# Score products of a cross-attention kernel: one row group per round takes 128 query rows at once

## The chip, the core and the metric

The kernel runs on one core of a Trainium2 chip. The metric is device time in microseconds (us) of that core for one execution. The kernel before takes 506.81 us, the median of three executions (506.36, 506.81 and 507.71).

## What is computed

One cross-attention layer with a residual and a layer norm, all in float32: 4 batches of 2048 query rows and 77 context rows, width 512, 16 heads of 32.

```python
qs  = (q @ wq).reshape(4, 2048, 16, 32).transpose(0, 2, 1, 3)
ks_ = (k @ wk).reshape(4,   77, 16, 32).transpose(0, 2, 1, 3)
vs  = (v @ wv).reshape(4,   77, 16, 32).transpose(0, 2, 1, 3)
scores = jnp.einsum('bhqd,bhkd->bhqk', qs, ks_) / jnp.sqrt(32.)
scores = jnp.where(mask[:, None, :, :], -jnp.inf, scores)
attn = jnp.einsum('bhqk,bhkd->bhqd', jax.nn.softmax(scores, -1), vs)
out  = attn.transpose(0, 2, 1, 3).reshape(4, 2048, 512) @ wo + q
out  = (out - mean) / jnp.sqrt(var + 1e-5) * gamma + beta
```

## The kernel before, in words

The 8192 query rows are cut into 64 tiles of 128 rows. Two tiles make a block, four tiles a group. For a group, TensorE (PE) makes the queries with `q_visit` (operand names pq<-xth, xtl; each product is three products of split high and low parts, rows L190 and L192). For a tile it makes the scores (`score`, L321, names sc<-kct,q). VectorE (DVE) adds the mask and finds each head's maximum (`maxima`, L364), ScalarE (ACT) takes the exponentials with their sums (`exps`, L379), GpSimd (POOL) divides by the sums (`normalise`, L390), DVE turns the probabilities by 32x32 squares (`transp`, L413), and DMAs regroup them (`regroup_part`, L425). PE then multiplies them with the values (`av`, L459, names pa<-PT,vsb) and the result with the output weights (`o_proj`, L564, names po<-woh, wol). What follows is the residual, the layer norm and the store.

The heads are 32 wide, so a query tile lies on PE's 128 contraction rows as four heads, each on its own 32 rows: a **row group**, `j` = 0 to 3. There are four such sets of heads, `g` = 0 to 3, so a tile has 4 x 4 scores of 128 query rows by 77 keys. In `score` the queries are the weights (loaded into the array), the keys are what streams through it. In the kernel before, each score is made in two products of 64 query rows, `half` = 0 and 64; each uses an array section of 32 rows by 64 columns, which the profile writes as 32*64. A **round** is one trip through the four row groups, with both halves: eight products. Because the data are float32, the trace has two loads and two MATMUL records for each product, so a round is 16 records, a tile 64 and a block 128.

Each engine runs its instructions in the order in which the program writes them. Nothing but two tables of words sets that order: the first six tiles come from a loop, the next 24 blocks (tiles 6 to 53) from `PAIR`, the last ten tiles from `ORDER`. A visit to the scores is one stretch on PE. For the 16 single tiles it is `scores`: four rounds. For the 24 blocks it is `scores_pair` (word S: six rounds) and `scores_rest` (word D: two rounds, their row groups taken as 0 and 2, then 3 and 1); but for the first of these blocks the two follow directly on each other on PE. Ahead of a block's visit PE does `av`, behind it `o_proj`.

The scores go to PSUM banks: one per row group for a single tile (sc_0 to sc_3), and for a block four of its own and two shared ones (sc_e, sc_f). DVE reads them from there.

Of the kernel before, what the change touches and what calls it, by code (L numbers as in the profile page):

```python
# [17 lines left out]
P = 128  # L18
# [8 lines left out]
GH = 4  # L27
# [49 lines left out]
def xattn_layernorm(  # L77
# [29 lines left out]
    def bank(name):  # L107
        while len(ring) % 8 in kept:
            ring.append(ring[-8])
        ring.append(ring[-8] if kept else ps.tile([P, 512], F32, tag="mm", name=name))  # L110
        return ring[-1]
# [49 lines left out]
    def keys_of(h):  # L161
        return slice(TAIL_K, NK2) if h % 2 == 0 else slice(0, NK)
# [145 lines left out]
    def scores(t):  # L308
        nmax[t] = sb.tile([P, H], F32, tag="nm", bufs=3, name=f"nm_{t}")
        sums[t] = sb.tile([P, H], F32, tag="sum", bufs=3, name=f"sum_{t}")  # L310
        sc = [bank(f"sc_{t}_{j}") for j in range(GH)]
        scs[t] = {(g, j): sc[j][:, g * NK : (g + 1) * NK] for g in range(NG) for j in range(GH)}
        for g in range(NG):
            for half in range(0, P, P // 2):
                for j in range(GH):
                    score(t, g, j, half, P // 2)

    def score(t, g, j, r0, n):
        q = slice(HD * j, HD * (j + 1))
        at = (t % 4) * P + r0  # L320
        nc.tensor.matmul(  # L321
            scs[t][g, j][r0 : r0 + n],
            qd[t // 4][q, g, at : at + n],
            kct[q, g, t // TPB, keys_of(j)],
            start=True,
            stop=True,
        )

    def scores_pair(b):
        for t in (2 * b, 2 * b + 1):  # L330
            nmax[t] = sb.tile([P, H], F32, tag="nm", bufs=3, name=f"nm_{t}")
            sums[t] = sb.tile([P, H], F32, tag="sum", bufs=3, name=f"sum_{t}")
            scs[t] = {}
        own = [bank(f"sc_{b}_{j}") for j in range(GH)]
        both = [bank(f"sc_{b}_{j}") for j in ("e", "f")]
        units = []
        for j in range(GH):
            mine = [(2 * b, g) for g in range(NG)] + [(2 * b + 1, g) for g in range(NG)]
            for i, (t, g) in enumerate(mine):
                bk, at = (own[j], i) if i < 6 else (both[j // 2], 2 * (j % 2) + i - 6)  # L340
                scs[t][g, j] = bk[:, at * NK : (at + 1) * NK]
            units.append(mine[6:] + mine[:6] if j % 2 == 0 else mine)
        for i in range(6):
            for half in range(0, P, P // 2):
                for j in range(GH):
                    score(*units[j][i], j, half, P // 2)
        held[b] = units

    def scores_rest(b):
        units = held.pop(b)  # L350
        for i in (6, 7):
            for js in ((0, 2), (3, 1)):
                for half in range(0, P, P // 2):
                    for j in js:
                        score(*units[j][i], j, half, P // 2)

    def maxima(t, lo, hi):
        pb = pbuf[t % NPB]
# [410 lines left out]
    for u in range(0, JOIN, 2):  # L769
# [6 lines left out]
        for t in (u - 4, u - 3):  # L776
            if t >= 0:
                load_x(t)
        scores(u)
        maxima(u, 0, H // 2)  # L780
        if u == 2:
# [53 lines left out]
        if u >= 4:  # L835
            av(n - 2)
            av_hi(n - 2, 0)
            av_hi(n - 2, 1)
        scores(u + 1)
        maxima(u + 1, 0, H // 4)  # L840
        if u >= 4:
# [42 lines left out]

    tile_ops = {
        "S": scores, "r": recip, "n": normalise, "t": transp, "W": av_tile, "x": load_x, "O": o_proj,
        "X": lambda t: resid(t, range(NC_D // 2 if t == NT - 1 else NC_D)), "+": residual, "u": rsqrt_one, "y": centre, "z": finish, "k": scale, "f": affine, "w": store,
        "v": bias_one, "K": stretch, "G": shift, "p": pool_scale, "I": act_mean, "J": act_squares, "M": keep,
# [48 lines left out]
    def pair(n):  # L937
        u = 2 * n
        words = PAIR.split()
        if n == JOIN // 2:  # L940
            words.remove("O-6")
            words.insert(words.index("D"), "O-6")
        for word in words:
            op, k, part, queue = read(word)
            if op == "S":
                scores_pair(n)
            elif op == "D":
                scores_rest(n)
            elif op in "LB":
                m, at = divmod(u, TPB)  # L950
                if m + 1 < NB and op == "L" and at == TPB - 10:
                    load_mask(m + 1)
                elif m + 1 < NB and op == "B" and at >= TPB - 8:
                    mask_quarter(m + 1, (at - TPB + 8) // 2)
            elif op == "P" and "." not in word:
                regroup(n + k)
            elif op in "Qq":
                if op == "Q" or divmod(2 * n + k, 4) in qp:
                    do(op, 2 * n + k)
            elif op in "gij":  # L960
                do(op, n + k)
            elif op in "PVab":
                if op in "PV" or n + k > JOIN // 2 - 3:
                    do(op, n + k, part, queue)
            elif u + k >= 0:
                do(op, u + k, part, queue)
# [54 lines left out]
```

## Time and profile before

| | |
|---|---|
| median of three executions | 506.81 us |
| the profiled execution's own time | 508.02 us |
| its span in the profile | 506.2 us |
| PE busy | 497.0 us (98%) |
| PE's weight loads (PEld) busy | 391.7 us (77%) |
| DVE, ACT, POOL busy | 463.0, 473.0, 427.6 us (91%, 93%, 84%) |
| records of the score products (L321) | 4096, in 58.48 us |

Busy time counts the stretches in which at least one instruction of an engine is under way; products overlap, so a busy PE need not be at its peak. A form such as 32*64 is the section of the array (contraction rows by weight columns), and what follows it is what streams (32 partitions by 77 elements). A line of the chain of waits is a share of the span on the path that ended last. PEclk is the share of TensorE's clock that was granted.

### The profile page before, as it was taken

Reading aid. Unit: us, or ns where it says so; the run is one execution under the profiler, and the core shown is the slowest. Engines: PE = TensorE matmul, PEld = TensorE weight load, DVE = VectorE, ACT = ScalarE, POOL = GpSimd, SP = SyncE. Lnnn points to the kernel's source line nnn. Section 1 sums busy time; section 2 is a strip of 40 time slices with the busy share of each in tenths; the row PEclk is TensorE's granted clock in tenths of the full one; section 3 lists DMA queues with packets and bytes.
Section 4 is the critical chain, followed back from the end, with each engine's and each line's share of the span. In section 5 each row is a group of like instructions: output and inputs, shape, how many; then the busy total and the mean of one; then the engine's idle time right before and its main releaser. Section 6 shows DMA issues by size and latency. Waiting matters only on the chain.

```text
span 506.2 us, 20441 instructions
## 1 busy us (share of the span) xinstructions
PE 497.0 (98%) x6908; PEld 391.7 (77%) x6908; DVE 463.0 (91%) x2567; ACT 473.0 (93%) x2240; POOL 427.6 (84%) x384
## 2 busy tenths in 40 slices
PE   9999999999999999999999999999999999999995
PEld 7987678777777877777787777778777777777784
DVE  6698899999989988999998998999999889999997
ACT  6798899999999999999999999999999999999971
POOL 0559367989988988989998888999988888999995
PEclk9999999999999999999999999999999999999998
DMA  8945867677887778878777877877778787677665
GB/s 314 388 168 149 222 187 194 190 196 202 231 229 218 223 201 219 229 209 229 213 219 211 232 199 223 229 224 227 216 196 221 199 247 235 170 189 222 167 210 208
DMA packets 58280, 109.50 MB, mean 216 GB/s; under 512 B 9203, under 2 KB 10739, under 8 KB 58176
## 3 DMA queue, kind: packets, MB, share of 16 engines
q1 hardware_dynamic: 55776, 103.35, 71.7%
q0 software_dynamic: 1872, 4.20, 2.8%
q8 instruction: 55, 0.90, 0.8%
q10 hardware_dynamic: 528, 0.66, 0.4%
q14 instruction: 49, 0.40, 0.3%
HBM read 41.68 MB, written 16.78 MB: 115 GB/s over the span
## 4 chain that ended last, share of the span: by engine, by line
PE 79%; DVE 8%; ACT 7%; DMA 2%; issue 1%; SPq 1%; POOL 0%; POOLq 0%; DVEq 0%; ACTq 0%
PE pq L192 27%; PE po L564 26%; PE pa L459 10%; ACT pbuf L379 7%; PE sc L321 6%; DVE B L413 2%; PE sc L564 2%; DVE pbuf L364 2%; PE sc_e L321 2%; PE pk L218 1%; PE pq L725 1%; PE pq L190 1%; PE sc_f L321 1%; SPq L425 1%; DMA out<-o 1%
## 5 line engine op out<-in xcount | busy, mean ns | idle before, releaser
L379 ACT ACTIVATE pbuf<-pbuf,nm 128x77 f32<-128x77 f32 x1024 | 352.6, 349 | 8.6 <-DVE nm L364 7.8
L379 ACT ACTIVATION_READ_ACCUMULATOR pbuf<-pbuf,nm 128x1 f32 x1024 | 193.9, 189 | 0.0
L390 POOL TENSOR_TENSOR pbuf<-pbuf,ri 128x1232 f32<-128x1232 f32 x63 | 145.9, 2316 | 20.8 <-DVE ri L385 17.4
L364 DVE CUSTOM_DVE_ANT_0 pbuf<-sc,mb 128x77 f32<-128x77 f32 x828 | 143.9, 231 | 6.9 <-PE sc L321 6.4
L192 PE MATMUL pq<-xtl,wqh 128*128 128x512 f32 (+1 forms) x256 | 98.3, 384 | 0.0
L192 PE MATMUL pq<-xth,wql 128*128 128x512 f32 (+1 forms) x256 | 98.2, 384 | 0.0
L413 DVE STREAM_TRANSPOSE B<-pbuf 128x1280 f32<-128x1280 f32 x63 | 94.6, 1503 | 0.4
L564 PE MATMUL po<-woh,AH 128*128 128x512 f32 x224 | 90.7, 405 | 0.0
L192 PE MATMUL pq<-xth,wqh 128*128 128x512 f32 (+1 forms) x230 | 88.6, 385 | 0.0
L564 PE MATMUL po<-wol,AH 128*128 128x512 f32 x224 | 87.3, 390 | 0.0
L592 POOL TENSOR_TENSOR o<-o,gam 128x512 f32<-128x512 f32 x53 | 68.7, 1295 | 21.5 <-ACT o L588 21.5
L564 PE MATMUL po<-woh,AL 128*128 128x512 f32 x224 | 86.5, 391 | 0.0
L364 DVE DVE_READ_ACCUMULATOR2_ANT nm<- 128x1 f32 x1024 | 84.4, 82 | 0.0
L593 POOL TENSOR_TENSOR o<-o,bet 128x512 f32<-128x512 f32 x53 | 68.3, 1289 | 4.2
L180 POOL TENSOR_TENSOR xtl<-xtf,xth 128x1024 fp32r<-128x1024 f32 x28 | 67.4, 2409 | 0.1
L459 PE MATMUL pa<-PT,vsb 96*32 96x256 f32 x960 | 58.2, 382 | 1.6 <-DVE vsb L267 1.0
L321 PE MATMUL sc<-kct,q 32*64 32x77 f32 x3312 | 56.0, 238 | 0.5 <-DVE q L209 0.5
L192 PEld LDWEIGHTS pq<-xth,wql 128*128 128x128 f32 x256 | 48.2, 188 | 8.4
L192 PEld LDWEIGHTS pq<-xtl,wqh 128*128 128x128 f32 x256 | 48.1, 188 | 8.4
L321 PEld LDWEIGHTS sc<-kct,q 32*64 32x64 f32 x3312 | 49.3, 130 | 6.5 <-issue 4.4
L564 PEld LDWEIGHTS po<-woh,AH 128*128 128x128 f32 x224 | 42.0, 188 | 10.7 <-DVE nm L364 0.4
L192 PEld LDWEIGHTS pq<-xth,wqh 128*128 128x128 f32 x230 | 43.2, 188 | 9.0
(191 smaller groups left out, 855.1 us busy)
## 6 DMA issues: line engine op xcount, KB each, us to landing
PT<-B SPq DMA_DIRECT2D x355, 128.0 KB
xtf<-xT SPq DMA_DIRECT2D x28, 512.0 KB
o<-x SPq DMA_DIRECT2D x56, 256.0 KB
out<-o SPq DMA_DIRECT2D x56, 256.0 KB
PT<-B POOLq DMA_DIRECT2D x16, 128.0 KB, 4.5
o_end<-x SPq DMA_DIRECT2D x7, 256.0 KB
out<-o_end SPq DMA_DIRECT2D x7, 256.0 KB
xtf<-xT SPq DMA_DIRECT2D x4, 256.0 KB
```

The costliest lines, as they stand in the source:

```text
L180: nc.gpsimd.tensor_tensor(l, fx.pop((g, c)), h.bitcast(F32), ALU.subtract)
L190: nc.tensor.matmul(pq[:, cols], wc, r[:, c, cols], start=False, stop=False)
L192: nc.tensor.matmul(pq, wc, r[:, c, rs], start=(n == 0), stop=(n == 11))
L321: nc.tensor.matmul(scs[t][g, j][r0 : r0 + n], qd[t // 4][q, g, at : at + n], kct[q, g, t // TPB, keys_of(j)], start=True, stop=True,)
L364: nc.vector.tensor_tensor_reduce(pb[:, i // 2, (i % 2) * NK : (i % 2 + 1) * NK], scs[t][g, j], mb[:, t % TPB, keys_of(h)], -1.0, CEIL, ALU ...
L379: nc.scalar.activation(p, p, AF.Exp, bias=nmax[t][:, i : i + 1], scale=-1.0, accum_out=sums[t][:, i : i + 1])
L390: nc.gpsimd.tensor_tensor(pv, pv, rv.to_broadcast((P, NP, 2, NK)), ALU.mult)
L413: nc.vector.transpose(bt.rearrange("p c q r -> p q c r"), pbuf[t % NPB].rearrange("p q (c r) -> p q c r", c=5),)
L459: nc.tensor.matmul(pas[b, g // 2][HD * j : HD * (j + 1), (g % 2) * BLK : (g % 2 + 1) * BLK], vsb[:, 2 * b // TPB, HD * h : HD * (h + 1)], ...
L564: nc.tensor.matmul(pos[t], a[:, c, rs], w[:, c], start=(first and n == 0), stop=(n == 11))
L592: nc.gpsimd.tensor_tensor(o, o, gam, ALU.mult)
L593: nc.gpsimd.tensor_tensor(o, o, bet, ALU.add)
```

## The change

In each round, one of the four row groups makes its score in one product with all 128 query rows as weights (a section of 32 rows by 128 columns) in place of the two halves. Which one moves on with the round: row group `j == g` for a single tile, `j == i % 4` for round `i` of a block. The product stands where the first half stood; the second half is left out. A round so has seven products in place of eight. What is multiplied and where it is written stay the same.

```diff
         for g in range(NG):
             for half in range(0, P, P // 2):
                 for j in range(GH):
-                    score(t, g, j, half, P // 2)
+                    score_part(t, g, j, half, j == g)
...
+    def score_part(t, g, j, half, whole):
+        if not whole:
+            score(t, g, j, half, P // 2)
+        elif half == 0:
+            score(t, g, j, 0, P)
...
         for i in range(6):
             for half in range(0, P, P // 2):
                 for j in range(GH):
-                    score(*units[j][i], j, half, P // 2)
+                    score_part(*units[j][i], j, half, j == i % GH)
...
             for js in ((0, 2), (3, 1)):
                 for half in range(0, P, P // 2):
                     for j in js:
-                        score(*units[j][i], j, half, P // 2)
+                        score_part(*units[j][i], j, half, j == i % GH)
```

On PE, a single tile's first two rounds stood so before (sc_0 to sc_3 are the banks of row groups 0 to 3; 64x77 is 64 weight columns and 77 streamed keys):

```order
L321 MATMUL sc_0_358<-kct,q_131 64x77 [waits Activation_49]
L321 MATMUL sc_1_359<-kct,q_131 64x77 [waits Activation_49]
L321 MATMUL sc_2_360<-kct,q_131 64x77
L321 MATMUL sc_3_361<-kct,q_131 64x77 [waits PE_49]
L321 MATMUL sc_0_358<-kct,q_131 64x77
L321 MATMUL sc_1_359<-kct,q_131 64x77
L321 MATMUL sc_2_360<-kct,q_131 64x77
L321 MATMUL sc_3_361<-kct,q_131 64x77
L321 MATMUL sc_0_358<-kct,q_131 64x77 [waits DVE_49]
L321 MATMUL sc_1_359<-kct,q_131 64x77 [waits DVE_49]
L321 MATMUL sc_2_360<-kct,q_131 64x77
L321 MATMUL sc_3_361<-kct,q_131 64x77
```

With the change, the same place, from the visit's first product into its third round:

```order
L321 MATMUL sc_0_358<-kct,q_131 128x77 [waits Activation_49]
L321 MATMUL sc_1_359<-kct,q_131 64x77 [waits Activation_49]
L321 MATMUL sc_2_360<-kct,q_131 64x77
L321 MATMUL sc_3_361<-kct,q_131 64x77 [waits PE_49]
L321 MATMUL sc_1_359<-kct,q_131 64x77
L321 MATMUL sc_2_360<-kct,q_131 64x77
L321 MATMUL sc_3_361<-kct,q_131 64x77
L321 MATMUL sc_0_358<-kct,q_131 64x77 [waits DVE_49]
L321 MATMUL sc_1_359<-kct,q_131 128x77 [waits DVE_49]
L321 MATMUL sc_2_360<-kct,q_131 64x77
L321 MATMUL sc_3_361<-kct,q_131 64x77
```

Seven products with 64 columns stand between one with 128 and the next. At the end of a block's visit, with the change (rounds 6 and 7 of `scores_rest` and the first product of `o_proj`, which is L570 there):

```order
L321 MATMUL sc_2_2883<-kct,q_2265 128x77
L321 MATMUL sc_0_2881<-kct,q_2265 64x77
L321 MATMUL sc_f<-kct,q_2265 64x77 [waits DVE_49]
L321 MATMUL sc_e<-kct,q_2265 64x77
L321 MATMUL sc_f<-kct,q_2265 64x77
L321 MATMUL sc_e<-kct,q_2265 64x77
L321 MATMUL sc_0_2881<-kct,q_2265 64x77
L321 MATMUL sc_2_2883<-kct,q_2265 64x77
L321 MATMUL sc_0_2881<-kct,q_2265 64x77
L321 MATMUL sc_2_2883<-kct,q_2265 64x77
L321 MATMUL sc_f<-kct,q_2265 128x77
L321 MATMUL sc_e<-kct,q_2265 64x77 x2
```

Here nine products with 64 columns stand between two with 128, and two behind the last. Over the whole program 256 products with 128 columns take the place of 512 with 64; PE goes from a 64-column product to a 128-column one 216 times, and back 256 times. On the other engines no instruction is added, removed or moved.

## The prediction

> **What bounds the kernel now.** I read the page's busy times and chain first, then the busy times of the steady stretch, then PE's waits.
>
> ```profile
> PE 497.0 (98%) x6908; PEld 391.7 (77%) x6908; DVE 463.0 (91%) x2567; ACT 473.0 (93%) x2240; POOL 427.6 (84%) x384
> PE 79%; DVE 8%; ACT 7%; DMA 2%; issue 1%; SPq 1%; POOL 0%; POOLq 0%; DVEq 0%; ACTq 0%
> ...
> 105.80:253.10 147.30, 147.30 (x2094) 115.48 (x2090) 137.73 (x786) 144.75 (x691) 133.46 (x111) 1.00 0.78 216
> ...
> PE pa L459 <- DVE vsb L267: 1.0, 1, 1.0
> PE pw L692 <- POOL ident L683: 0.9, 1, 0.9
> PE sc L321 <- DVE q L209: 0.5, 1, 0.5
> PE pa L459 <- DVE ri L385: 0.3, 1, 0.3
> ```
>
> PE holds 79% of the chain. The third row is ten block periods (columns: PE, PEld, DVE, ACT, POOL): PE never rests, ACT (fourth) leaves 2.55 us, 0.255 us a period. Over the whole run PE waits 1.8 us for DVE (three rows; pw is the warm-up). So whatever a score visit costs on PE, the kernel pays nearly in full; what it saves, up to 0.255 us a block, before ACT is as full as PE.
>
> What the visits cost now, by the busy times of the score products alone (columns: PE, PEld) over the span and over 21 block visits, and a single tile's visit in the timeline (columns: start, time from the first start to the last end, count):
>
> ```profile
> 0.00:506.20 506.20, 58.48 (x4096) 51.91 (x4096) 1.00 0.76 216
> 91.00:400.00 309.00, 37.50 (x2688) 34.22 (x2688) 1.00 0.78 217
> ...
> 418.58 0.39 PE L564 MATMUL po<-woh,AL 128*128 128x512 f32 x1
> 418.90 0.95 PE L321 MATMUL sc<-kct,q 32*64 32x77 f32 x64
> 419.78 0.50 PE L192 MATMUL pq<-xth,wqh 128*128 128x512 f32 x1
> 420.11 0.39 PE L192 MATMUL pq<-xtl,wqh 128*128 128x512 f32 x1
> ...
> L321 PE MATMUL sc<-kct,q x3312: 222/225/277, 20.9 to 471.6; 32*64 32x77 f32 x195
> ```
>
> A single visit takes 0.88 us from its first start to the next work's (418.90 to 419.78). Its last record starts at 418.90 + 0.95 - 0.225 (last row, median), so 0.155 us pass from the last score's start to the first start in the next form. Busy time runs 0.225 - 0.155 = 0.07 us past that; a block's visit is 37.50 / 21 - 0.07 = 1.72 us. All visits: 16 x 0.88 + 24 x 1.72 = 55 us. That is all there is to gain from.
>
> **What a change of form costs.** The question is what happens between 32*64 and 32*128, which no row of this trace shows. Other changes of form it shows in plenty:
>
> ```profile
> 252.79 0.38 PE L459 MATMUL pa<-PT,vsb 96*32 96x256 f32 x1
> 253.10 0.28 PE L321 MATMUL sc_e<-kct,q 32*64 32x77 f32 x1
> ...
> 253.15 0.28 PE L321 MATMUL sc<-kct,q 32*64 32x77 f32 x1
> 253.22 0.23 PE L321 MATMUL sc_e<-kct,q 32*64 32x77 f32 x1
> ...
> 253.27 0.23 PE L321 MATMUL sc<-kct,q 32*64 32x77 f32 x1
> 253.29 0.23 PE L321 MATMUL sc_e<-kct,q 32*64 32x77 f32 x1
> ...
> 483.85 0.38 PE L459 MATMUL pa<-PT,vsb 96*32 96x256 f32 x1
> 484.15 0.44 PE L439 MATMUL pa<-ident,pbuf 128*77 128x128 f32 x2
> ...
> 492.73 0.27 PE L492 MATMUL po<-PT,vsb 96*32 96x128 f32 x1
> 492.82 0.28 PE L474 MATMUL sc<-PT,vsb 77*32 77x128 f32 x1
> ```
>
> Within one form, eight scores on eight sections start 0.007 us apart (253.10 to 253.15, eight starts), the second pass of the same product comes 0.12 later (253.22), the next product on that section 0.065 after that (253.29): a pass streams 0.065. When the form changes, nothing overlaps: 0.155 from the last start is 0.065 of streaming and 0.09 in which PE starts nothing. From pa to the scores it is 0.31. At 483.85 the columns go from 32 to 77 and the rows from 96 to 128, both sides float32: again 0.30. At 492.73 the rows go from 96 to 77 and the columns stay 32: 0.09, no gap. So the gap follows the columns of the section, and 64 to 128 of them at equal rows is such a change. [...]
>
> Behind a gap the first load is bare too: the first MATMUL of a 32*64 stretch takes 0.277 against 0.225, so 0.05, that of 128 columns 0.50 against 0.39 (rows at 419.78 and 420.11), so 0.11.
>
> **The price of a round, step by step.** The 128-column product (W): load 0.11, then its second load, streaming of the second pass, gap. The loads follow each other at once here:
>
> ```profile
> 419.78 0.19 PEld L192 LDWEIGHTS pq<-xth,wqh 128*128 128x128 f32 x1
> 419.88 0.19 PEld L192 LDWEIGHTS pq<-xtl,wqh 128*128 128x128 f32 x1
> ```
>
> The second load starts 0.10 behind the first, while the first product still streams through the same rows. Two loads of 0.10 to 0.11 let W's second pass start 0.215 after its first load, and 0.155 later the halves may load: 0.37 for W. I bound it by 0.275 (loads as short as the 0.05 of 64 columns: 0.05 + 0.07 + 0.155) and 0.43 (second load only after the first pass, 0.065 more). I take 0.37, from the rows with 128 columns. [...]
>
> Seven halves: all on different sections, so second passes start from 0.12 on, the last at 0.12 + 6 x 0.007 = 0.16, and 0.155 later W may load: 0.315. Bounds: 0.27 (no spacing) and 0.40 (products let in at the visit's average, 1.72 / 64 = 0.027 each: 7 x 0.027 + 0.05 + 0.155). Likewise 0.28 for two halves, 0.29 for three, 0.31 for six; nine use one section twice, 0.41.
>
> A single tile: four W, three times seven halves, then three: 4 x 0.37 + 3 x 0.315 + 0.29 = 2.72 in place of 0.88, +1.84. A block: eight W, and 7, 7, 7, 3, 7, 6, 9, 2 halves: 2.96 + 4 x 0.315 + 0.29 + 0.31 + 0.41 + 0.28 = 5.51 in place of 1.72, +3.79. The eight saved products are in that. Sum: 16 x 1.84 + 24 x 3.79 = 29.4 + 91.0 = 120.4. PE's waits of 1.8 for DVE may take up to that much; I subtract 1.8. It all lies on PE, which has no other cover; a block's 14.7 us period becomes 18.5, and ACT, DVE and POOL, which were close behind, get slack. Maxima start later by part of the visit, but the exponentials behind them have that slack. The waits stand on the same products as before; a W that writes a bank waits for DVE once in place of twice. DMA issues do not move.
>
> Against the profiled execution's 508.0: 508.0 + 118.6 = 626.6. It was 1.2 above the median, so **625 us**. With the lower bounds a tile is 2.2 (+1.3) and a block 4.4 (+2.7), 85.6 less 1.8: 591. With the upper, 3.1 (+2.2) and 6.5 (+4.8): 150, 657.
>
> **Rivals.**
>
> No gap between these two forms (faster). For it: rows stay 32 wide, and no row shows this pair; halves run out of each other's order as if sections were independent. A visit then only loses records, 16 of 128 in a block (1.72 / 8 = 0.215) and 8 of 64 in a single (0.11): 24 x 0.215 + 16 x 0.11 = 6.9 us, 500 us. ACT's 0.255 a block just allows that. Against: 483.85, where columns alone made the gap.
>
> The gap is local: W waits for its own row group, the other three go on. For it: each form change in the trace involves sections that share rows, so none shows whether unshared rows wait. Then one row group sets the pace: over a single tile, three rounds of 0.13 and one W of 0.37 with 0.09 ahead and a bare load of 0.05 behind: 0.90 against 0.88. A block: 6 x 0.13 + 2 x 0.51 = 1.80 against 1.72. 16 x 0.02 + 24 x 0.08 = 2.2: 509 us, no change or a little slower. Against: the first scores at 253.10 need 64 of the columns, yet none starts before all of pa is through.
>
> The clock: PE streams less in visits three times as long and its clock is cut.
>
> ```profile
> 492.00:494.00 2.00, 2.00 (x65) 1.80 (x66) 2.00 (x4) 1.53 (x4) 1.84 (x4) 1.00 0.58 223
> 502.00:504.00 2.00, 0.00 (x0) 0.00 (x0) 0.60 (x2) 0.00 (x0) 0.90 (x1) 0.84 0.43 152
> 504.00:506.20 2.20, 0.00 (x0) 0.00 (x0) 0.00 (x0) 0.00 (x0) 0.00 (x0) 0.50 0.26 101
> ```
>
> The clock falls to 0.50 only where PE has nothing for some four us; with small products and form changes (492 to 494) it stays at 1.00. If visits of 5.51 and 2.72 ran with loads and streams, about half their time, at half the clock, that is some 24 x 2.75 + 16 x 1.35 = 88 more, 713 us.
>
> **How the numbers follow.** Forecast (a gap at each of 472 changes, 625): 0.80. No gap, 500: 0.08. Local, 509: 0.08, half of it within 0.3% either way, a quarter each side. Clock, 713: 0.04. About 0.3% is what a measurement of this kernel can tell from no change. Faster 0.08 + 0.02 = 0.10; same 0.04; slower 0.80 + 0.02 + 0.04 = 0.86. The forecast's range is 591 to 657; what I may have mis-sized in both W and the halves at once widens it to 580 to 665, which leaves out the rivals, 0.20.
>
> **What would show it.** The changed profile has a form 32*128 with 77 streamed elements, 512 records. Right: some 0.155 between the last 32*64 start and the 32*128 start, 0.37 from there to the next 32*64 load, single visits of 2.7 and block visits of 5.5 us, PE's share of the chain above 79%, ACT's busy share down to some 75%, PEclk still 9s. Wrong: a 32*128 product that starts 0.007 us behind a half (no gap), halves of other row groups starting while W streams (local), PEclk digits below 9 (clock), or visits in this form and yet a time near 507, which would say that PE did not set it.

## The result, and the profile after

The change takes 725.43 us (median of four runs, 723.07 to 726.03) against 507.23 for the kernel before on the same chip: 1.430 times as long, 95% interval 1.426 to 1.434. The forecast was 625 with a range of 580 to 665: the sign was right, the size was not. The rival by which the clock is cut had been put at 713, with a chance of 0.04.

The page after, its busy times, its two rows on the clock and DMA in 40 slices, and the chain by engine and by line:

```profile
PE 716.7 (99%) x6396; PEld 543.2 (75%) x6396; DVE 469.7 (65%) x2567; ACT 480.0 (66%) x2240; POOL 424.1 (59%) x384
...
PEclk9999987887878878789878788787888879797999
...
PE 96%; DVE 1%; ACT 1%; DMA 0%; issue 0%; POOL 0%; POOLq 0%
PE po L570 29%; PE sc L321 24%; PE pq L192 24%; PE pa L465 8%; PE sc_f L321 3%; PE sc_e L321 3%; PE sc L570 2%; PE pv L258 1%; PE pk L218 1%; PE pq L731 1%; PE pq L190 1%; DMA xtf<-xT 0%; DVE st L608 0%; DVE o_end L573 0%; DVE AL L518 0%
```

PE carries 96% of the chain, up from 79%, and the other engines do the same work in a longer span. The digits of PEclk, all 9s before but the last, are mostly 7s and 8s here: over the span the granted clock was 0.841.

A single visit in the timeline:

```profile
602.83 0.40 PE L465 MATMUL pa<-PT,vsb 96*32 96x256 f32 x4
603.16 2.78 PE L321 MATMUL sc<-kct,q 32*128 32x77 f32 x56
605.87 0.50 PE L570 MATMUL po<-woh,AH 128*128 128x512 f32 x1
```

The same visit, the one block visit that ran at full clock, and another block visit, as busy times of the score products with the clock they were granted (columns: us, PE, PEld, PEclk, DMA share, GB/s):

```profile
603.16:605.87 2.71, 2.71 (x56) 2.05 (x56) 1.00 0.45 114
338.16:343.66 5.50, 5.50 (x112) 4.17 (x112) 1.00 0.60 167
316.69:323.61 6.92, 6.92 (x112) 5.20 (x112) 0.74 0.63 189
```

At full clock a single visit takes 2.71 us (forecast 2.72) and a block visit 5.50 (forecast 5.51). Most block visits took 6.7 to 7.5, because the clock was halved under them: it stood at 0.50 for 3.0 to 5.1 us of each. Behind the visit the halved clock reaches into the output products, which are not changed at all; they start 0.42 and 0.43 us apart and then, with the clock back, 0.24:

```profile
305.27 0.63 PE L570 MATMUL po<-woh,AH 128*128 128x512 f32 x1
305.69 0.63 PE L570 MATMUL po<-wol,AH 128*128 128x512 f32 x1
306.12 0.54 PE L570 MATMUL po<-woh,AL 128*128 128x512 f32 x1
306.50 0.40 PE L570 MATMUL po<-woh,AH 128*128 128x512 f32 x1
306.74 0.40 PE L570 MATMUL po<-wol,AH 128*128 128x512 f32 x1
```

So the loss can be added up from the two traces. I sum the time from each visit's first score to the first start of other work, 41 visits in each trace, and call what is left of the span the rest:

| us | before | change | change, all visits at full clock |
|---|---|---|---|
| visits | 57.0 | 214.6 | 24 x 5.495 + 16 x 2.707 = 175.2 |
| rest of the span | 449.2 | 509.2 | |
| span | 506.2 | 723.8 | |

The changes of form cost 175.2 - 57.0 = 118.2 us. The clock cost 214.6 - 175.2 = 39.4 inside the visits and 509.2 - 449.2 = 60.0 outside them, 99.4 in all. Together that is the 217.6 by which the span grew.

Where the clock falls is seen in equal stretches across the visit that starts at 316.69 (columns: us, PE, PEld, DVE, ACT, POOL, PEclk, DMA share, GB/s):

```profile
313.25:316.66 3.41, 3.41 (x40) 1.96 (x38) 2.39 (x4) 2.60 (x11) 2.45 (x5) 1.00 0.34 80
316.66:320.08 3.42, 3.42 (x77) 2.57 (x73) 0.85 (x3) 2.02 (x3) 3.42 (x3) 1.00 0.39 121
320.08:323.49 3.41, 3.41 (x48) 2.63 (x40) 1.95 (x17) 1.48 (x8) 3.41 (x2) 0.50 0.88 262
323.49:326.90 3.41, 3.41 (x12) 2.62 (x9) 3.17 (x27) 2.83 (x17) 1.38 (x2) 0.50 0.23 85
326.90:330.32 3.42, 3.42 (x17) 2.79 (x16) 2.02 (x14) 3.42 (x21) 0.00 (x0) 1.00 0.45 104
```

The clock shows 1.00 and 0.50 here, nothing between, and changes at multiples of 3.41 us: the stretches at half clock last 3.41, 6.83 or 10.24. The first stretch filled by the visit still has the full clock; the next has half, and it comes back only after a stretch of dense products, 323.49 to 326.90. In all five rows PE is "busy" for 100% of the time, so in these rows the clock fell without idle PE in the profile.

### The profile page after: what moved, and what is told of

Its sections match the earlier page's. It is cut to its first block, busy times and chain, and to the rows that moved or that the text cites. A ratio compares the mean times of both kernels' runs of the same rounds, so it can differ in the third digit from the quotient of the medians.

```text
span 723.8 us, 19385 instructions
## 1 busy us (share of the span) xinstructions
PE 716.7 (99%) x6396; PEld 543.2 (75%) x6396; DVE 469.7 (65%) x2567; ACT 480.0 (66%) x2240; POOL 424.1 (59%) x384
## 4 chain that ended last, share of the span: by engine, by line
PE 96%; DVE 1%; ACT 1%; DMA 0%; issue 0%; POOL 0%; POOLq 0%
PE po L570 29%; PE sc L321 24%; PE pq L192 24%; PE pa L465 8%; PE sc_f L321 3%; PE sc_e L321 3%; PE sc L570 2%; PE pv L258 1%; PE pk L218 1%; PE pq L731 1%; PE pq L190 1%; DMA xtf<-xT 0%; DVE st L608 0%; DVE o_end L573 0%; DVE AL L518 0%
## 5 line engine op out<-in xcount | busy, mean ns | idle before, releaser
L321 PE MATMUL sc<-kct,q 32*64 32x77 f32 (+1 forms) x2898 | 183.1, 291 | 0.0
L321 PEld LDWEIGHTS sc<-kct,q 32*64 32x64 f32 (+1 forms) x2898 | 134.6, 160 | 46.5 <-issue 12.4
L570 PE MATMUL po<-woh,AH 128*128 128x512 f32 x224 | 112.7, 503 | 0.0
L570 PE MATMUL po<-wol,AH 128*128 128x512 f32 x224 | 106.5, 476 | 0.0
L570 PE MATMUL po<-woh,AL 128*128 128x512 f32 x224 | 103.4, 466 | 0.0
L573 DVE TENSOR_TENSOR o<-po,o 128x512 f32<-128x512 f32 x56 | 38.7, 691 | 62.7 <-PE po L570 62.7
L570 PEld LDWEIGHTS po<-woh,AH 128*128 128x128 f32 x224 | 55.2, 247 | 17.2 <-issue 3.7
L570 PEld LDWEIGHTS po<-woh,AL 128*128 128x128 f32 x224 | 53.7, 240 | 13.6
L570 PEld LDWEIGHTS po<-wol,AH 128*128 128x128 f32 x224 | 55.1, 246 | 11.7
L514 ACT CAST AH<-pa 128x512 fp32r<-128x512 f32 x60 | 34.7, 580 | 41.9 <-PE pa L465 41.9
```

Source lines behind the costliest of these rows:

```text
L321: nc.tensor.matmul(scs[t][g, j][r0 : r0 + n], qd[t // 4][q, g, at : at + n], kct[q, g, t // TPB, keys_of(j)], start=True, stop=True,)
L570: nc.tensor.matmul(pos[t], a[:, c, rs], w[:, c], start=(first and n == 0), stop=(n == 11))
L573: nc.vector.tensor_tensor(od[t], pos.pop(t), od[t], ALU.add)
```

## The experiments

The theory was by now: a change of the section's form costs a gap and a bare load, and a visit stretched by gaps gives the array so little to do for 3.4 us that the clock is halved. The rivals: a product with 128 columns is dear by itself; the clock is cut by the form changes as such; only gaps in the stream cut it.

**All scores whole.** The halves are left out; four 128-column products a round, no form change inside a visit.

```diff
     def score_part(t, g, j, half, whole):
-        if not whole:
-            score(t, g, j, half, P // 2)
-        elif half == 0:
+        if half == 0:
             score(t, g, j, 0, P)
```

> Every score is one product of 128 query rows; no halves, so no form change inside a visit. Theory (a change of the section's columns costs a gap and a bare load, and long thin visits cost the clock): both costs are gone; a row group loads 2 x 0.107 us per product, so a block visit is about 1.87 us and a single one about 1.0; 508 to 520 us, likeliest 514, granted clock above 0.99. Rival (a product with 128 columns is dear by itself, 0.37 each as in the change, wherever it stands): 512 x 0.37 less 55 of visits now, 640 us.

Measured: 514.26 us, 1.0145 of before (1.013 to 1.016), clock 0.997. A single visit in its timeline:

```profile
420.53 1.13 PE L321 MATMUL sc<-kct,q 32*128 32x77 f32 x32
421.59 0.50 PE L568 MATMUL po<-woh,AH 128*128 128x512 f32 x1
```

It takes 1.06 us, a block visit 1.95. The 128-column product is not dear: twice as many of them as in the change cost 7 us, not 218. It is a little slower than two halves: on each row group the records with 128 columns now start one behind the other, 0.11 us apart by the trace (136.46, 136.57 and 136.69 in a block visit).

**The same products, whole ones together.** As many of both kinds as in the change, but a visit's whole ones stand in one run: 64 added form changes in place of 472.

```diff
         for i in range(6):
+            score(*units[i % GH][i], i % GH, 0, P)
+        for i in range(6):
             for half in range(0, P, P // 2):
                 for j in range(GH):
-                    score_part(*units[j][i], j, half, j == i % GH)
+                    if j != i % GH:
+                        score(*units[j][i], j, half, P // 2)
```

(The same in `scores`; in `scores_rest` the two whole ones come last.)

> The change's 256 whole products and 1536 halves, but the whole ones of a visit stand together (first in a single visit and in a block's first part, last in its second part), so 64 form changes are added in place of 472. Theory: single visit about 1.12 us, block visit about 2.3 us, 515 to 535 us, likeliest 525, clock above 0.99. Rival (the 128-column product itself is what costs): as many of them as in the change, at 0.37 less what they replace, 590 to 630 us.

Measured: 525.41 us, 1.0368 of before (1.0351 to 1.0386), clock 0.998. A block visit from its whole products to its first halves, and its end:

```profile
199.91 0.33 PE L324 MATMUL sc_e<-kct,q 32*128 32x77 f32 x1
199.92 0.34 PE L324 MATMUL sc<-kct,q 32*128 32x77 f32 x3
...
200.52 0.28 PE L324 MATMUL sc_f<-kct,q 32*64 32x77 f32 x1
...
202.01 0.27 PE L324 MATMUL sc_f<-kct,q 32*128 32x77 f32 x1
202.21 0.50 PE L579 MATMUL po<-woh,AH 128*128 128x512 f32 x1
```

2.30 us, where the same products in the change's order take 5.50. The order alone, and with it the number of form changes, makes the difference.

**Dense work inside the visits.** The change with four dense products, whose results nobody uses, after rounds 2 and 5 of a block and round 1 of a single tile (`wq_f` is a part of the query weights, read as float32).

```diff
+    def fill(bk):
+        for _ in range(4):
+            nc.tensor.matmul(bk[:, 4 * NK :], wq_f[:, :P], wq_f[:, : 512 - 4 * NK], start=True, stop=True)
...
                     score_part(*units[j][i], j, half, j == i % GH)
+            if i in (2, 5):
+                fill(both[0])
```

> The change as it is, plus four dense float32 products (128 rows, 128 columns, 204 streamed) after rounds 2 and 5 of a block visit and after round 1 of a single one, results unused. 64 such breaks, some 1.85 us each at full clock, 118 us in all; the 472 form changes stay and 128 more come. Theory (the clock is cut because a stretch of some 3.4 us holds too little work for the array): the stretches are broken, granted clock above 0.97, and the time is 627 + 118, about 745 us. Rival (the clock is cut by the form changes themselves, by their number): clock at or below 0.85 as in the change, 830 us or more.

Measured: 742.90 us, 1.466 of before, clock 0.998. One break:

```profile
282.89 0.36 PE L324 MATMUL sc<-kct,q 32*64 32x77 f32 x8
283.18 1.65 PE L340 MATMUL sc_e<-wqh 128*128 128x204 f32 x8
284.76 0.36 PE L324 MATMUL sc<-kct,q 32*64 32x77 f32 x6
```

All the change's form changes are still there, and 128 more, and the clock stays full. So their number does not cut the clock. That thin stretches cut it fits: what is gone here is only the stretches without dense work. The visits take 292.9 us here and the rest 448.1, as in the kernel before: the 60 us outside the visits are gone. 111 us of breaks (64, each 1.73 from the last score ahead to the first behind) more than eat up the 99 that the clock gives back, so the run is 17 us longer than the change.

**Every second round.** The whole product only where `g` or `i` is even.

```diff
-                    score_part(t, g, j, half, j == g)
+                    score_part(t, g, j, half, j == g and g % 2 == 0)
...
-                    score_part(*units[j][i], j, half, j == i % GH)
+                    score_part(*units[j][i], j, half, j == i % GH and i % 2 == 0)
```

> The whole product only in every second round: 128 in place of 256, 216 added form changes in place of 472. Theory: a single visit about 1.6 us, a block visit about 3.2, so 508 + 48 = 556 us at full clock, and the visits are too short to fill a 3.4 us stretch, so the clock stays above 0.97. Rival (clock lost in proportion to form changes): clock about 0.93, 600 us.

Measured: 570.58 us, 1.126 of before, clock 0.975. A single visit takes 1.71 and a block visit 3.33, each 0.1 over what I worked out. The clock of 0.975 is within the theory's bound (above 0.97; the rival had 0.93), but the time lies between the theory's 556 and the rival's 600: the clock did fall, though at eight places only. One such place (columns as above):

```profile
195.49:198.90 3.41, 3.41 (x41) 2.11 (x39) 2.67 (x4) 3.09 (x15) 2.01 (x6) 1.00 0.89 204
198.90:202.31 3.41, 3.41 (x128) 2.62 (x120) 1.38 (x10) 2.40 (x5) 3.33 (x3) 1.00 0.75 201
202.31:205.73 3.42, 3.42 (x30) 2.59 (x14) 3.42 (x40) 3.04 (x19) 3.42 (x3) 0.50 0.92 245
205.73:209.14 3.41, 3.41 (x17) 2.81 (x16) 3.00 (x16) 3.41 (x22) 2.15 (x2) 1.00 0.42 163
```

The second row holds all 120 score records of a visit: it lay in step with one stretch of the clock. The eight stretches that were followed by half clock hold 102 to 120 score records each. Those with 94 or fewer, where a visit is split between two stretches, kept the clock, and so did one with 118. My "too short to fill a stretch" was wrong by the eight.

**One section alone, without form changes.** The kernel before, with 40 products on one 32*64 section in each block visit, results unused.

```diff
                     score(*units[j][i], j, half, P // 2)
+            if i == 5:
+                for _ in range(40):
+                    nc.tensor.matmul(own[0][:64, 6 * NK :], wq_f[:32, :64], wq_f[:32, : 512 - 6 * NK], start=True, stop=True)
```

> The kernel before the change, plus 40 products in each block's first visit part on one 32*64 section alone (50 streamed, results unused): no form change, PE streams or loads without a gap, but on an eighth of the array, some 4.3 us a block, 102 us in all at full clock. Theory that the clock follows how much of the array works: clock cut, 0.90 or below, 650 us or more. Rival that it follows whether PE streams at all (gaps are what cuts it): clock above 0.98, about 610 us.

Measured: 655.95 us, 1.294 of before (1.287 to 1.302), clock 0.922. At full clock a block visit takes 6.08, 4.36 more than the 1.72 of before, so some 105 of the 149 us are the products and some 45 the clock. Across one such visit:

```profile
208.40:211.80 3.40, 3.40 (x142) 2.60 (x133) 1.72 (x11) 2.67 (x5) 3.32 (x3) 1.00 0.26 79
211.80:215.20 3.40, 3.40 (x62) 3.40 (x61) 1.37 (x11) 1.42 (x9) 3.40 (x3) 1.00 0.94 276
215.20:218.60 3.40, 3.40 (x46) 2.85 (x45) 1.77 (x23) 1.44 (x9) 2.38 (x2) 0.50 0.22 79
```

In the second row PE multiplies or loads without a pause (3.40 us of 3.40, by the profile) and changes no form, and the clock falls to 0.50 behind it. So streaming without a pause did not keep the clock here; that the work was on one section in eight fits the theory.

**Quarters in place of the whole.** In the same places, the first half as two products of 32 queries (32*32) and the second half as it was: no section has 128 columns.

```diff
         elif half == 0:
-            score(t, g, j, 0, P)
+            score(t, g, j, 0, 32)
+            score(t, g, j, 32, 32)
+        else:
+            score(t, g, j, half, P // 2)
```

> In place of the change's product of 128 query rows, the same row group makes its first half as two products of 32 (sections 32*32) and its second half as one of 64; nothing has 128 columns. Theory (any change of the section's columns costs the gap): a quarter pair takes about 0.25 us from load to next load, seven halves 0.315, so a single visit about 2.2 us, a block visit about 4.5, 508 + 89 = 597 us at full clock; the array's share in a visit is some 0.23, so the clock is cut too and the time is 630 to 690, granted clock 0.86 to 0.92. Rival (the gap belongs to sections that take the full 128 columns): no gap, visits as before and some more products, 505 to 520 us, clock above 0.99.

Measured: 623.16 us, 1.230 of before (1.226 to 1.234), clock 0.948. A block visit at full clock:

```profile
168.41 0.32 PE L321 MATMUL sc_e<-kct,q 32*32 32x77 f32 x4
168.66 0.28 PE L321 MATMUL sc<-kct,q 32*64 32x77 f32 x1
...
172.86 0.23 PE L321 MATMUL sc_e<-kct,q 32*64 32x77 f32 x1
173.01 0.50 PE L573 MATMUL po<-woh,AH 128*128 128x512 f32 x1
```

0.25 from the quarters to the halves, as expected, and 4.60 for the visit (4.5 expected): narrowing the columns costs the gap too. The clock cost some 27 us (623 less 506 and 24 x 4.60 + 16 x 2.26 - 57 = 90), and was cut less often than I expected: the clock of 0.948 is above the 0.86 to 0.92 of the theory, and the time below its 630 to 690.

**Rows alone.** The kernel before, with four products on a 64*64 section between the two parts of a block visit, results unused.

```diff
+            if i == 5:
+                for _ in range(4):
+                    nc.tensor.matmul(own[0][:64, 6 * NK :], wq_f[:64, :64], wq_f[:64, : 512 - 6 * NK], start=True, stop=True)
```

> The kernel before, plus four products on a 64*64 section (50 streamed, results unused) between the first and second part of each block visit: the section's rows change from 32 to 64 and back, its columns stay 64. If a change of rows alone costs the same gap: 0.155 from the last score's start to the first added one, a bare load there and back, some 0.8 us a block, 522 to 530 us. If only columns count: the added products start within 0.02 us of the last score and cost some 0.4 us a block, 512 to 520 us.

Measured: 526.9 us, 1.0403 of before (1.0348 to 1.0457). The place:

```profile
217.35 0.49 PE L322 MATMUL sc<-kct,q 32*64 32x77 f32 x24
217.77 0.66 PE L350 MATMUL sc<-wqh 64*64 64x50 f32 x8
218.36 0.30 PE L322 MATMUL sc<-kct,q 32*64 32x77 f32 x4
```

The last score starts at 217.35 + 0.49 - 0.225 = 217.615, the first added product 0.155 later. Rows alone cost the same gap. "The gap follows the columns", as the prediction had it, is too narrow.

## Why the prediction was right in its sum and wrong in its time

**What bounds the kernel**: right. PE went from 79% to 96% of the chain, and what the visits cost more was paid in full.

**What a change of form costs**: right in kind and size. At full clock the whole product starts 0.155 us behind the last half's start in all 145 such places of the trace. The halves of other row groups do not start while a whole product is under way (the first starts 0.37 behind it in the rows below), so the gap holds for the whole array and the local rival is out; so is the rival without a gap. The one correction is that rows count as well, though not every change of them: 96 to 77 cost nothing in the kernel before (0.09 from start to start), 32 to 64 cost the whole gap (0.155).

**The price of a round**: right. Single visit 2.71 for 2.72, block visit 5.50 for 5.51, sum 118.2 for 118.6. The choice of 0.37 for the whole product was the right one: in the timeline of a single visit it is 0.37 from its first pass to the halves' first (the second row runs from these halves into the next whole product).

```profile
603.16 0.33 PE L321 MATMUL sc<-kct,q 32*128 32x77 f32 x1
...
603.53 0.64 PE L321 MATMUL sc<-kct,q 32*64 32x77 f32 x15
```

By the starts in the trace its second load begins 0.11 behind its first, as assumed, and seven halves take 0.31 to the next whole product (0.315 forecast). Within the 0.37 the split is another: 0.17 passes from the first pass to the second and 0.20 from there to the halves, where the prediction had 0.215 and 0.155. The sum holds and its two parts do not; why is open.

**The clock**: this is the step that failed. The forecast's sum has no term for the clock, and 99.4 us were measured. What kept the term out is the rival's "falls to 0.50 only where PE has nothing for some four us" and its chance of 0.04. The row I leaned on against it, 492 to 494, spans 2 us, less than one stretch of the clock; and the profile of before could not show a thin stretch, because it has none while PE works. Counting each MATMUL record's streaming time by its section's share of the array (an estimate: 0.065 us for 77 float32 elements, others in proportion, half of that for the products of split parts, which start 0.23 apart at 512 elements), the thinnest 3.41 us of the kernel before, from its first scores to its last product, holds 0.46 of what the array can do. The same count could have been made for the forecast's own visit: 96 records of 0.065 on an eighth of the array and 16 on a quarter are 1.04 us of full array, and spread over 5.51 us that is 0.19. The prediction named thin visits as a rival and put 88 us on them (99 measured), and then let rows of a kernel without thin stretches set the chance. That 88 comes near 99 is luck: it was worked out for the visits alone, where the clock cost 39.4; the other 60.0 lay behind them, where the rival had nothing.

What share cuts the clock isn't settled. By that count, in stretches laid on the boundaries that the clock's own records give, full-clock stretches of the change that were followed by half clock hold 0.19 to 0.34, the others 0.33 and more; with every second round it is 0.30 to 0.33 against 0.34 and more; with the dense breaks nothing is under 0.38 and nothing is cut. With the quarters the edge lies lower (cut from 0.24 to 0.30, kept from 0.28), and so it does with one section alone (cut from 0.09 to 0.27, kept from 0.27). So within each kernel the count parts the two sets but for 0.02 at most, and between kernels the edge moves from 0.27 to 0.34: a small share goes with the cut in every one of them, but no one share parts all of them. Counting only the time in which any product streams parts them worse: with one section alone the clock was cut behind stretches that stream for up to 0.74 of their time, and with the dense breaks it was kept behind one of 0.63.

## What to carry to other kernels

Keep products of one section form together on PE: here 0.155 us passed from the last start with 64 columns to the first with 128 and 0.20 on the way back, where neighbours of one form start 0.007 apart, and 64 steps in place of 472 turned 218 us of loss into 19, with the same products. When a forecast stretches a dense phase with gaps, count how much of the array works in 3.4 us, the length of one stretch of the clock in this trace; the trace of before has no such thin stretch while PE works, and it said nothing on whether the clock would hold. And look beyond the changed phase: 60 of the 99 us that the clock cost were paid by products that nobody had touched.

## What the runs showed that I had not expected

By the profile the clock fell with PE busy for 100% of the time, and with no gap in its work where only one section in eight was in use (0.922 over that run). A change of rows alone, 32 to 64 at equal columns, cost the same 0.155 us from the last start to the next as the change from 64 columns to 128. And once cut, the clock stayed at half for one to three stretches of 3.41 us, dense products included, so one thin visit, 5.5 us long at full clock, could bring up to 10.24 us at half clock.
